# A decoder layer on one core: a written order changed in cross-attention, and 64 tokens laid out twice

## The chip, the core and the metric

The kernel runs on one core of a Trainium2 chip. A core has a matrix engine (TensorE, PE in the profile, with its weight loads shown apart as PEld), a vector engine (VectorE, DVE), a scalar engine (ScalarE, ACT), a general engine (GpSimd, POOL) and SyncE (SP), which here only issues transfers (DMAs). Each engine works through its own queue in order; semaphores make one wait for another. The metric is the device time of one execution in microseconds (us); lower is better.

## The reference

A post-norm decoder layer on 32 sequences of 64 tokens, so 2048 tokens of 512 features, all in float32:

```python
x = layernorm(x + attn(x))            # 32 heads, 8 key/value heads, head size 128
x = layernorm(x + xattn(x, ctx))      # the same head counts, keys and values from ctx
x = layernorm(x + ffn(x))             # z = x W + b, plus a clamped low-rank part

def attn(x):
    q, k, v = x @ wq.T, x @ wk.T, x @ wv.T         # rope on q and k, one angle set for all tokens
    k_full = concat([k_cache[block_idx], k[0]])    # 512 cached keys, then the 64 of sequence 0
    v_full = concat([v_cache[block_idx], v[0]])
    return softmax(q @ k_full.T / sqrt(128)) @ v_full @ wo.T

def xattn(x, ctx):                                 # per sequence, 64 queries by 64 keys
    q = x @ Wq + bq
    k, v = split(ctx @ Wkv + bkv)
    return softmax(q @ k.T / sqrt(128)) @ v @ Wo + bo
```

Two facts matter here: in self-attention every query sees the new keys and values of the first sequence alone (`k[0]`, `v[0]`), and cross-attention ends with the bias `bo`, added before the second layer norm.

## The kernel before

Tokens are worked on in four blocks of 512 (`tb` 0 to 3). The residual stream of a block lies in SBUF as `acc[tb]`, token rows by features, in four tiles of 128 rows; its transpose, features by tokens, is `xT[tb]`. Most matrix products of 512 by 512 by 512 are done in Strassen's manner (Winograd's form): seven products of quarter size instead of eight, numbered 1 to 7, each made by `Product.mul` as eight TensorE instructions of 256 columns (L318). The sums that go into them are made on POOL (`left_sums`, `right_sums`, `token_sums`, `output_sums`); the sums that come out are made on DVE as products leave PSUM, the matrix engine's output memory. Products share PSUM banks x, y and z, so that product 7, which adds to the bank of product 6, has to wait until DVE has read product 6 (L359), and product 4 waits for the read of product 7 (L363). The last reads of a query block add the bias (L339).

**Self-attention** goes through groups g = 0 to 7 of key/value heads, in each through the four blocks, in each through four heads. Its order on PE, DVE and ACT is that of the written program. For each group `new_keys` (L618 on) makes the keys and values of the first sequence. The keys take four matmuls of `wk` by `x64`, the 64 tokens of the first sequence, features by tokens (L628). The values are wanted twice, on partitions 0 to 63 and on 64 to 127 of one bank, since they are used in pairs of heads with half of the array each; so `x64` is the weights side of eight matmuls (L634), four feature chunks times two halves of the output partitions. (Each float32 matmul shows as two instructions in the trace, so 16 in a call.) `x64` is copied out of the first block's transpose once at the start, on POOL (L820). `cached_keys` (L648) and the score matmuls (L667) come behind `new_keys` on PE.

**The key/value stage** makes the keys and values of the context for all of cross-attention, in four passes `gp` over four blocks, seven products each (L426, L432; DVE reads L443). PE and DVE follow the written order; POOL, ACT and SP are placed by the scheduler. Between the products a list `fill` is worked off, one entry after each product: the statistics and scaling of the first layer norm in pass 1, and from pass 2 the turning of `acc` into `xT`, four DVE transposes a block (`turn_rows`, L149) and 16 small transfers (`move_rows`, L156). Empty entries space the blocks out.

**Cross-attention** goes through 32 units, `units[n] = (g, tb)`, eight groups by four blocks. PE, POOL and DVE follow the written order (until the last unit, from which DVE is placed by the scheduler). The loop from L1347 does in iteration n, in this order:

- the queries of unit n: products 1, 6, 5, 7, 2, 4, 3, each followed by its DVE read, with pending scalings (`scales`) let in behind the read of product 6, and the token sums for unit n + 1 on POOL (`next_tokens`, L1317 to L1322);
- what is pending from a layer norm (`scales`, then `later`, which turns a finished block), with `a_turn` putting single transposes between products;
- `attend(n - 1)`: weighted values (L1191), which need the transposed softmax weights `pTx` that eight transfers of `move(n - 1)` (L1169, on SP) bring; their eviction, half by ACT (L1210) and half by DVE (L1212); `output_sums` on POOL (L289 to L295);
- `scores(n)` (L1119), the largest score (L1128);
- in group 0 alone, the bias: four POOL adds of `bo` to `acc[tb]` (L1398), one for each tile of 128 rows;
- the output projection of unit n - 1, products 1, 5, 6, 3, 7, 2, 4 (L318, DVE reads L387 and L395), with the softmax steps of unit n between them: exponentials (L1135, L1136), denominators (L1140), weights (a reciprocal L1144 and a multiply L1145, for halves 0 and 1), then the turn of both halves (L1155) and `move(n)`;
- with the last block of a group, `load_xq(g + 1)`: loads of the next query weights and their four sums on POOL (L223 to L226).

In unit 0 there is no projection, so its softmax stands alone between its scores and unit 1's queries. In group 7 the projection of a block is its last, and `layernorm_parts` follows at once (L1223 on): `stats()` makes the statistics on DVE (L173 to L175) and the square root on ACT (L176); `scale`, left in `scales`, makes a reciprocal and a shift on DVE (L187, L189) and scales the four tiles on ACT (L191).

Of the kernel before, what the change touches and what calls it, by code (L numbers as in the profile page):

```python
# [9 lines left out]
F32 = mybir.dt.float32  # L10
I32 = mybir.dt.int32
AF = mybir.ActivationFunctionType
ALU = mybir.AluOpType
# [3 lines left out]
P = 128  # L17
# [4 lines left out]
SEQ = 64  # L22
TB = 512
NTB = NT // TB
TPB = TB // P
NC = DIM // P
# [26 lines left out]
def decoder_layer(  # L53
# [30 lines left out]
    nc = tc.nc  # L84
# [431 lines left out]
    with ExitStack() as ph:  # L516
# [97 lines left out]
            nc.vector.tensor_tensor(k4[:, :, :, 0], k4[:, :, :, 0], tmp, ALU.add)  # L614


        x64 = kc.tile([P, NC, SEQ], F32, name="x64")

        def new_keys(g):

            wk, wv = wkv_cur.pop(g)
            kTs[g] = kv.tile([P, NKEY], F32, tag="kT", name=f"kT{g}")
            new = bank([P, 1, TB], f"new{g}", "po1")[:, 0, :]
            pk, pv = new[:, :SEQ], new[:, P : 2 * P]
            for c in range(NC):
                nc.tensor.matmul(  # L628
                    pk, wk[:, c, :], x64[:, c, :], start=(c == 0), stop=(c == NC - 1),
                    skip_group_check=True,  # L630
                )
            for c in range(NC):
                for i in range(2):
                    nc.tensor.matmul(  # L634
                        pv[i * SEQ : (i + 1) * SEQ, :], x64[:, c, :], wv[:, c, :],
                        start=False, stop=(c == NC - 1), skip_group_check=True,
                    )
            nc.scalar.activation(
                kTs[g].rearrange("p (s b k) -> p s b k", s=2, k=SQ)[:, :, SHARED, :],
                pk.rearrange("p (s k) -> p s k", s=2), AF.Copy, scale=nrm2,  # L640
            )
            nc.scalar.copy(vs[g][:, NKT, :], pv)
# [174 lines left out]
        t = {i: big.tile([P, 2, HF], F32, tag=f"tx{i}", name=f"tx0_{i}") for i in range(1, 5)}  # L817
        for j in range(NKT):
            gather_keys(0, j)
        nc.gpsimd.tensor_copy(  # L820
            x64.rearrange("p c (j k) -> p c j k", j=TPB),
            xTs[0].rearrange("p c (j k) -> p c j k", j=TPB)[:, :, :, : SEQ // TPB],
        )
        nc.vector.tensor_tensor(t[1], q[0, 1], q[0, 0], sub)
        nc.vector.tensor_tensor(wq0[7], wq0[1], wq0[5], sub)
        nc.vector.tensor_tensor(wq0[5], wq0[5], wq0[4], ALU.add)
# [187 lines left out]
    with ExitStack() as ph:  # L1014
# [23 lines left out]
        with ExitStack() as st:  # L1038
            ke = st.enter_context(tc.tile_pool(name="ke", bufs=1))
            psum.append(st.enter_context(tc.tile_pool(name="kps", bufs=1, space=PSUM)))  # L1040
            st.enter_context(tc.manual_schedule(
                engines={mybir.EngineType.PE, mybir.EngineType.DVE}
            ))
            for tb in range(2, NTB):
                encT[tb] = ke.tile([P, NC, TB], F32, tag=f"encT{tb}", name=f"encT{tb}")
                load_features(encT[tb], encT_in, tb)
            kvw[1] = load_kv_left(1, "wo")
            fill = []

            pairs = [(gp, tb) for gp in range(NKV // 2) for tb in range(NTB)][1:]  # L1050
            for k, (gp, tb) in enumerate(pairs):
                if gp == 1:
                    stats, scale = layernorm_parts(tb, "a")
                    fill += [lambda: None, stats, lambda: None, scale]
                if gp == 2:
                    room = ke.tile([P, DIM // SQ, SQ, TPB], F32, tag="room", name=f"room{tb}")
                    fill += [lambda tb=tb, j=j, room=room: turn_rows(
                        acc[tb][:, j, :], room, j) for j in range(TPB)]
                    fill.append(lambda tb=tb, room=room: move_rows(room, xT[tb]))

                    fill += [lambda: None] * 7
                tiles = [ke.tile([P, 2, 2, HF], F32, tag=f"c{i}", name=f"c{gp}_{tb}_{i}", bufs=2)
                         for i in range(2)]
                pr = keys_values(gp, tb, tiles, {z: f"{z}{k % 2}" for z in "xyz"})
                for i in KV_ORDER:
                    pr.step(i)
                    pr.read()
                    if fill:
                        fill.pop(0)()
                if gp == 0 and tb < NTB - 1:  # L1070
                    encR[tb + 1] = token_sums(
                        encT[tb + 1], f"te{tb + 1}", nc.gpsimd, ke, f"te{tb + 1}_"
                    )
                store_kv(gp, tb, tiles)
                if tb == NTB - 1 and gp < 2:
                    kvw[gp + 2] = load_kv_left(gp + 2, ("wq", "wo")[gp])
                if tb == NTB - 1 and gp == 2:
                    load_xq(0)
                if gp == 3 and tb == 0:
                    right[0] = token_sums(xT[0], "txx0", nc.gpsimd)  # L1080
            load_xo(0)
            psum.pop()
# [134 lines left out]
        def project(n, *steps):  # L1217
            g, tb = units[n]
            for i in steps:
                pjs[n].step(i)  # L1220
                pjs[n].read()
            if steps[-1] == 4:
                del pjs[n]  # L1223
                if g == NKV - 1:
                    stats, scale = layernorm_parts(tb, "x", by_act=True)
                    stats()
                    scales.append(scale)
                    if tb < 2:
                        later.append(lambda: turn_block(tb))
                    else:  # L1230
                        later.append(lambda: transpose_block(tb, "x2"))
# [104 lines left out]
        def parts(n, *made):  # L1336

            for part, pr in made:
                if n < N:
                    part(n, pr)  # L1340

        def steps(n, *made):
            if n >= 0:
                project(n, *made)

        mxs, es, dens, scales = {}, {}, {}, []
        for n in range(N + 1):  # L1347
            if n == N - 1:

                units_order.close()  # L1350
                ph.enter_context(tc.manual_schedule(
                    engines={mybir.EngineType.PE, mybir.EngineType.Pool}
                ))
            if n < N:
                g, tb = units[n]
                q = queries(n)
                for i in (1, 6, 5, 7):
                    q.step(i)
                    q.read()
                    while scales and i == 6:  # L1360
                        scales.pop(0)()
                q.corner()
                q.step(2)


                behind = g > 0 and tb == 1
                if not behind:
                    next_tokens(n + 1, 0)
            while scales:
                scales.pop(0)()  # L1370
            while later:
                later.pop(0)()
            if n < N:
                a_turn()
                q.step(4)
                q.read()
                a_turn()
                q.step(3)
                q.read()
                a_turn()  # L1380


            if n > 0:
                attend(n - 1)
            if n < N:
                if n + 1 < N:
                    load_kv(n + 1)
                scores(n)
                if behind:
                    next_tokens(n + 1, 0)  # L1390
                next_tokens(n + 1, 1)
            if n == N:
                feed_forward(1)
            parts(n, (largest, 0), (largest, 1))
            if n < N and g == 0:
                for j in range(TPB):
                    a = acc[tb][:, j, :]
                    nc.gpsimd.tensor_tensor(a, a, bo, ALU.add)  # L1398
            steps(n - 1, 1, 5)
            parts(n, (exponentials, 0))  # L1400
            steps(n - 1, 6)
            parts(n, (exponentials, 1), (denominators, 0))
            a_turn()
            steps(n - 1, 3)
            parts(n, (denominators, 1))
            if n < N and tb == NTB - 1 and g + 1 < NKV:
                load_xq(g + 1)
            steps(n - 1, 7)
            parts(n, (weights, 0))
            steps(n - 1, 2)  # L1410
            parts(n, (weights, 1))
            if n > 0:
                steps(n - 1, 4)
                parts(n, (turn, 0), (turn, 1))
                if n < N:
                    move(n)
                if n < N and tb == 0:
                    if g > 0:
                        load_xo(g)
                    if g == NKV - 1:  # L1420
                        load_ffn()
            if n == 0:
                parts(n, (turn, 0), (turn, 1))
                move(n)
            if n == N - 1:
                feed_forward(0)
        scales.pop(0)()
# [51 lines left out]
```

## Time and profile before

| what | us |
|---|---|
| three runs | 3034.66, 3035.4, 3037.62 (median 3035.4) |
| the profiled execution | 3034.3 |
| its span, first to last instruction | 3032.2 |
| PE busy | 3005.9 |
| DVE busy | 2187.9 |
| POOL busy | 961.5 |
| ACT busy | 801.7 |

By time: self-attention ends near 1838, the key/value stage runs to 2023, cross-attention to about 2980, where it overlaps with the feed-forward network that ends the kernel. The granted TensorE clock is 0.999 of full speed. A line of the wait view names the engine and line that waited, what it waited for, the total, the number of times and the longest. A line of the chain view gives start, duration, engine, tile and line. A line of the timeline has start, duration, engine, line, operation, tiles and shapes, and in brackets how long the engine had idled before it and for whom. All starts are in us from the beginning of the span. Instructions of one engine overlap a little, so the distance between two starts, not the duration, tells what one costs: a quarter product of eight instructions is 1.89 from first start to last end and 1.73 from start to start.

### The profile page before, as it was taken

To read this page: it belongs to the slowest core of one execution; us is meant where nothing else is said; L and a number is where in the kernel's file an instruction comes from. 1 tells how busy PE (TensorE), PEld (TensorE's weight loads), DVE (VectorE), ACT (ScalarE), POOL (GpSimd) and SP (SyncE) were. 2 spreads that over 40 slices of the span, in tenths; PEclk is the share of its full clock that TensorE was granted. 3 is DMA by queue.
4 is the path that set the end of the run, shared out by engine and by line. 5 is a ranking of instruction groups with operands and counts; after the bars stand their busy time and mean duration, and the time that the engine had idled before them with its cause. 6 is when DMAs were issued, how large, how long until landed. Compare 5 with 4: busy or idle time off the path is not lost.

```text
span 3032.2 us, 42610 instructions
## 1 busy us (share of the span) xinstructions
PE 3005.9 (99%) x14848; PEld 2318.4 (76%) x14848; DVE 2187.9 (72%) x4045; ACT 801.7 (26%) x1916; POOL 961.5 (32%) x798
## 2 busy tenths in 40 slices
PE   8999999999999999999999999999999999999998
PEld 6777777777777777777777768988888888888875
DVE  6787777777877877877877863547666666666787
ACT  4322222222232332232232231111111111111233
POOL 5222321321321321321321223035444444444320
PEclk9999999999999999999999999999999999999999
DMA  6454444444444444444444344341121121121121
GB/s 182 129 133 126 114 111 126 114 110 126 113 111 126 112 112 125 111 113 127 109 115 116 93 132 146 129 145 54 50 67 53 52 66 51 56 63 50 55 58 42
DMA packets 216084, 304.99 MB, mean 101 GB/s; under 512 B 47424, under 2 KB 110400, under 8 KB 215872
## 3 DMA queue, kind: packets, MB, share of 16 engines
q1 hardware_dynamic: 201584, 286.91, 34.7%
q10 hardware_dynamic: 11472, 9.46, 1.0%
q0 software_dynamic: 2816, 5.90, 0.7%
q8 instruction: 120, 1.97, 0.3%
q14 instruction: 92, 0.75, 0.1%
HBM read 107.05 MB, written 20.97 MB: 42 GB/s over the span
## 4 chain that ended last, share of the span: by engine, by line
PE 96%; DVE 2%; DMA 1%; POOL 0%; ACT 0%; issue 0%; ACTq 0%; DVEq 0%; POOLq 0%
PE po L718 16%; PE s L667 16%; PE sx L1119 2%; PE pox L1191 2%; PE w_1y L318 1%; PE q_3y L318 1%; PE w_0y L318 1%; PE w_3y L318 1%; PE q_1y L318 1%; PE q_0y L318 1%; PE qx_0y L318 1%; PE wx_0y L318 1%; PE qx_3y L318 1%; PE wx_3y L318 1%; PE wx_1y L318 1%; PE q_2y L318 1%
## 5 line engine op out<-in xcount | busy, mean ns | idle before, releaser
L675 ACT ACTIVATE p<-s,nmax 128x576 f32<-128x576 f32 x512 | 379.1, 740 | 1211.3 <-DVE nmax L672 1166.6
L667 PE MATMUL s<-kT,qT 128*128 128x288 f32 x2048 | 575.3, 407 | 0.5 <-ACT p L675 0.5
L718 PE MATMUL po<-pT,v 128*128 128x512 f32 (+1 forms) x1280 | 549.1, 602 | 2.5 <-DMA wv<-in_wvT 1.4
L667 PEld LDWEIGHTS s<-kT,qT 128*128 128x128 f32 x2048 | 387.7, 190 | 101.6 <-issue 19.7
L672 DVE TENSOR_REDUCE nmax<-s 128x1 f32<-128x576 f32 x512 | 383.5, 749 | 60.6 <-PE s L667 59.6
L698 DVE STREAM_TRANSPOSE T<-p 128x576 f32<-128x576 f32 x512 | 393.9, 769 | 11.7 <-ACT p L688 7.4
L718 PEld LDWEIGHTS po<-pT,v 128*128 128x128 f32 (+1 forms) x1280 | 213.3, 189 | 202.5 <-issue 175.3
L690 DVE TENSOR_SCALAR p<-p,den 128x576 f32<-128x576 f32 x488 | 305.3, 626 | 17.1
L684 DVE RECIPROCAL den<-den 128x1 f32<-128x1 f32 x512 | 83.8, 164 | 225.7 <-ACT p L675 214.2
L289 POOL TENSOR_TENSOR so<-oT,oT 128x512 f32<-128x512 f32 x32 | 40.7, 1272 | 543.3 <-ACT oT L741 543.3
L292 POOL TENSOR_TENSOR so<-oT 128x512 f32<-128x512 f32 x32 | 40.6, 1270 | 310.3 <-PE w_1y L318 92.8
L289 POOL TENSOR_TENSOR sox<-oTx,oTx 128x512 f32<-128x512 f32 x32 | 40.5, 1266 | 296.8 <-ACT oTx L1210 210.5
L1210 ACT ACTIVATE oTx<-pox,bv 128x128 f32<-128x128 f32 x256 | 73.7, 488 | 117.2 <-PE pox L1191 117.2
L230 POOL TENSOR_TENSOR tx<-xT 128x512 f32<-128x512 f32 x31 | 40.5, 1306 | 197.5 <-PE q_3z L318 63.3
L675 ACT ACTIVATION_READ_ACCUMULATOR p<-s,nmax 128x1 f32 x512 | 98.7, 193 | 0.0
L1320 POOL TENSOR_TENSOR txx<-x1T 128x512 f32<-128x512 f32 x31 | 39.3, 1268 | 175.1 <-PE qx_3z L318 75.3
L1136 ACT ACTIVATE ex<-ex 128x512 f32<-128x512 f32 x64 | 40.3, 630 | 202.2 <-DVE ex L1135 202.2
L1212 DVE TENSOR_SCALAR oTx<-pox,bv 128x128 f32<-128x128 f32 x256 | 72.6, 421 | 8.5 <-PE pox L1191 8.5
L1119 PEld LDWEIGHTS sx<-kvx,qTx 128*64 128x64 f32 x2048 | 62.3, 138 | 10.6 <-issue 10.6
L741 ACT COPY oT<-po 128x512 f32<-128x512 f32 x128 | 68.2, 586 | 4.5 <-PE po L718 4.1
L1119 PE MATMUL sx<-kvx,qTx 128*64 128x64 f32 x2048 | 66.7, 224 | 0.0
L1191 PE MATMUL pox<-pTx,kvx 64*128 64x256 f32 x512 | 64.6, 389 | 0.3 <-DMA pTx<-Tx 0.3
(445 smaller groups left out, 5773.1 us busy)
## 6 DMA issues: line engine op xcount, KB each, us to landing
pT<-T SPq DMA_DIRECT2D x1016, 80.0 KB
pT<-T SPq DMA_DIRECT2D x1008, 64.0 KB
xT<-in_xT SPq DMA_DIRECT2D x123, 256.0 KB
kvx<-kv SPq DMA_DIRECT2D x32, 512.0 KB
pTx<-Tx SPq DMA_DIRECT2D x256, 64.0 KB
kv<-c SPq DMA_DIRECT2D x30, 512.0 KB
wo<-in_woT SPq DMA_DIRECT2D x32, 256.0 KB
xwq<-in_xwq SPq DMA_DIRECT2D x32, 256.0 KB
```

What stands on the lines that cost most here:

```text
L289: nc.gpsimd.tensor_tensor(t[1], a[1, 0], a[1, 1], ALU.add)
L318: nc.tensor.matmul(self.banks[b][:, m, :], self.left[i][:, k, m * P : (m + 1) * P], self.right[i][:, k, :], start=(first and m + k == 0), ...
L667: nc.tensor.matmul(s[:, a, :HALF], qTs[n // REP][:, units[n][2], i * P : (i + 1) * P], kTs[g][:, a * HALF : (a + 1) * HALF], start=True, s ...
L672: nc.vector.tensor_reduce(nmax, s[:, :, :HALF], AX.XY, ALU.max, negate=True)
L675: nc.scalar.activation(p.rearrange("q (a k) -> q a k", a=2), s[:, :, :HALF], AF.Exp, bias=nmax, accum_out=den,)
L684: nc.vector.reciprocal(den, den)
L690: nc.vector.tensor_scalar(p, p, den, None, ALU.mult)
L698: nc.vector.transpose(Ts[n][:, :, i, :], ps_.pop((n, i)).rearrange("q (b k) -> q b k", k=SQ))
L718: nc.tensor.matmul(pos[n].rearrange("d (a q) -> d a q", a=NQD), vs[units[n][0]][rows, v, :], pTs[n // 2][rows, :, chunk, :], skip_group_ch ...
L1119: nc.tensor.matmul(s[b * SEQ : (b + 1) * SEQ, i * REP + h, :], qTs[n][:, h, pr * HF + c0 : pr * HF + c0 + SEQ], kvs[n][:, pr, 0, c0 : c0 + ...
L1191: nc.tensor.matmul(po[pr, b][:, i, :].rearrange("d (h a j) -> d h a j", h=REP, a=2), kvs[n][r, pr, 1, i * HD : (i + 1) * HD], pTs[n][r, :, ...
L1210: nc.scalar.activation(dst, src, AF.Identity, bias=bias)
```

## The change

Four things change, none of which alters what is computed.

1. The tokens of the first sequence lie twice in `x128`, side by side, copied by two POOL copies. The new values are then four matmuls with 128 columns of weights, whose output fills all 128 partitions, instead of eight with 64.
2. The bias adds go from units 0 to 3 of cross-attention into the `fill` list of the key/value stage, one entry for a block's four adds, right behind the transfers that move the block's transpose. An empty entry makes room for it.
3. In unit 0 the second half of the weights step, both turns and `move(0)` are put into a list `due`, which is worked off in unit 1 behind the DVE read of product 6.
4. In group 7 the statistics of block 0 go into `due` too, so they run in unit 30 behind the read of product 6; the scalings of all blocks are no longer let in at that place and run behind product 2, where the loop has emptied `scales` all along.

In the changed program's built order, DVE differs at two places (units 1 and 30), ACT at one (in unit 30 the eviction L354 goes ahead of the scaling L191), POOL in the second copy and the 16 adds, and SP nowhere.

```diff
-        x64 = kc.tile([P, NC, SEQ], F32, name="x64")
+        x128 = kc.tile([P, NC, 2 * SEQ], F32, name="x128")
+        x64 = x128[:, :, :SEQ]
...
             for c in range(NC):
-                for i in range(2):
-                    nc.tensor.matmul(
-                        pv[i * SEQ : (i + 1) * SEQ, :], x64[:, c, :], wv[:, c, :],
-                        start=False, stop=(c == NC - 1), skip_group_check=True,
-                    )
+                nc.tensor.matmul(
+                    pv, x128[:, c, :], wv[:, c, :],
+                    start=False, stop=(c == NC - 1), skip_group_check=True,
+                )
...
-        nc.gpsimd.tensor_copy(
-            x64.rearrange("p c (j k) -> p c j k", j=TPB),
-            xTs[0].rearrange("p c (j k) -> p c j k", j=TPB)[:, :, :, : SEQ // TPB],
-        )
+        for i in range(2):
+            nc.gpsimd.tensor_copy(
+                x128[:, :, i * SEQ : (i + 1) * SEQ].rearrange("p c (j k) -> p c j k", j=TPB),
+                xTs[0].rearrange("p c (j k) -> p c j k", j=TPB)[:, :, :, : SEQ // TPB],
+            )
...
+            def add_bias(tb):
+                for j in range(TPB):
+                    a = acc[tb][:, j, :]
+                    nc.gpsimd.tensor_tensor(a, a, bo, ALU.add)
...
                     fill.append(lambda tb=tb, room=room: move_rows(room, xT[tb]))
+                    fill.append(lambda tb=tb: add_bias(tb))
-                    fill += [lambda: None] * 7
+                    fill += [lambda: None] * 6
...
                     stats, scale = layernorm_parts(tb, "x", by_act=True)
-                    stats()
+                    if tb == 0:
+                        due.append(stats)
+                    else:
+                        stats()
                     scales.append(scale)
...
+        due = []
         mxs, es, dens, scales = {}, {}, {}, []
...
                 for i in (1, 6, 5, 7):
                     q.step(i)
                     q.read()
-                    while scales and i == 6:
-                        scales.pop(0)()
+                    while due and i == 6:
+                        due.pop(0)()
...
             parts(n, (largest, 0), (largest, 1))
-            if n < N and g == 0:
-                for j in range(TPB):
-                    a = acc[tb][:, j, :]
-                    nc.gpsimd.tensor_tensor(a, a, bo, ALU.add)
             steps(n - 1, 1, 5)
...
             steps(n - 1, 2)
-            parts(n, (weights, 1))
             if n > 0:
+                parts(n, (weights, 1))
                 steps(n - 1, 4)
...
             if n == 0:
-                parts(n, (turn, 0), (turn, 1))
-                move(n)
+                due += [lambda: parts(0, (weights, 1), (turn, 0), (turn, 1)), lambda: move(0)]
```

## The prediction

> **What bounds the kernel now.** I read the busy times first, then the chain of work that ended last, then PE's waits from the start of cross-attention on.
>
> ```profile
> PE 3005.9 (99%) x14848; PEld 2318.4 (76%) x14848; DVE 2187.9 (72%) x4045; ACT 801.7 (26%) x1916; POOL 961.5 (32%) x798
> PE 96%; DVE 2%; DMA 1%; POOL 0%; ACT 0%; issue 0%; ACTq 0%; DVEq 0%; POOLq 0%
> PE qx_0y L318 <- POOL xwq L225: 1.8, 1, 1.8
> PE qx_1y L318 <- DVE qTx L359: 1.5, 1, 1.5
> PE qx_2y L318 <- DVE rstd_x L187: 1.2, 1, 1.2
> ```
>
> TensorE is the bound nearly everywhere: other engines matter only where PE stands still. In 1000 us of cross-attention and feed-forward it stands still three times for more than a microsecond, and the change has one edit for each. The fourth edit shortens PE's own work, in self-attention. So the sum has four terms, each a place on PE's line.
>
> **Term A, new values with full width (new_keys).** Eight calls, seven in steady state. In the chain, one of them reads (start, duration, what):
>
> ```profile
> 1243.89 0.97 PE s L667 x4
> 1246.59 0.84 PE new L628 x8
> 1247.42 1.02 PE new L634 x16
> 1248.45 1.17 PE s L667 x4
> 1997.09 0.89 PE kv_1z L432 x8
> ```
>
> The sixteen half-wide instructions of L634 (64 columns of weights) take 1.02 us. The score matmuls right behind them take 1.17, where the same four take 0.97 elsewhere: leaving the half-wide form costs 0.20. After the change there are eight instructions of 128x128 weights by 128 columns; the row of exactly that shape is the last one, 0.89 for eight, with no change of form on either side. Gain per call 1.02 - 0.89 + 1.17 - 0.97 = 0.33 us. In the first call the instructions behind are four transposes, 0.59 there against 4 x 0.11 = 0.44 in later groups, so 0.28. Sum 7 x 0.33 + 0.28 = 2.6 us. PE has no wait at these places, so all of it counts; bounds 0 (the form makes no difference; a loss is excluded by the 0.89 row, which no half-wide row undercuts) and 8 x 0.33 = 2.7. The second POOL copy costs another 0.79 (L820's duration) between 9.9 and 13.0 us, where POOL idles 3.08 us for gathered keys; PE first reads the copy at 15.1. Without that idle it would delay the key rotation by 0.79 at most.
>
> The Trainium skill, "TensorEngine Tiling (Array Packing)", section Theoretical Speedup, speaks against this edit: a side of at most 64 lets two tiles work at once, up to 2x. By that the halves already filled the array and A would be the 0.20 behind them alone, some 1.5 us in all; the rows give sixteen halves 1.02 against 0.89 and so bear it out for most of the time, not all.
>
> **Term B, the bias adds leave POOL's queue.** Sixteen adds of 1.27 us (L1398), four in each of units 0 to 3. In unit 3 they stand ahead of the four sums for the next query weights:
>
> ```profile
> 2118.43 4.95 POOL L1398 TENSOR_TENSOR acc<-acc,bo 128x512 f32<-128x512 f32 x4
> 2126.83 1.26 POOL L225 TENSOR_TENSOR xwq<-xwq,xwq 128x512 f32<-128x512 f32 x1
> 2128.14 1.99 PE L318 MATMUL qx_0y<-txx,xwq 128*128 128x256 f32 x8 [1.75 <-POOL xwq L225]
> ```
>
> PE's products follow each other every 1.73 us; the one before started at 2124.50 and the one after at 2129.98, so the stop cost 5.48 - 2 x 1.727 = 2.03 us. Without the adds L225 ends near 2122, 4 us ahead of need; the weights' transfers were issued at 2105 to 2107 and the transfer engines are quiet by 2110. Next in line is unit 4's weighted-value product, whose transposed weights land near 2134.5 against a need at 2136.7: covered. B = 2.0 (bounds 1.9 to 2.1). In their new place, the key/value stage, the adds take 16 x 1.27 = 20.3 us of a POOL that idles there in three stretches of about 40 us. Behind them in POOL's new order stand weight sums and the first token sums; the latter ended at 1985.3 and are read at 2025. Each add waits for the DVE transposes of its block, all done by 1996.2; DVE touches acc again at 2057.8. Cost 0; were POOL not idle, 20 us less that slack of 40.
>
> **Term C, unit 0's second half of the softmax behind the first read of unit 1.** Today:
>
> ```profile
> 2042.65 1.30 DVE L1155 STREAM_TRANSPOSE Tx<-ex 128x512 f32<-128x512 f32 x2
> 2043.87 0.65 DVE L359 TENSOR_TENSOR qTx<-qx_1y,qTx 128x512 f32<-128x512 f32 x1
> 2043.97 5.21 SPq L1169 DMA_DIRECT2D pTx<-Tx  x8
> 2044.67 1.97 PE L318 MATMUL qx_1y<-txx,xwq 128*128 128x256 f32 x8 [1.55 <-DVE qTx L359]
> 2051.74 2.00 PE L1191 MATMUL pox<-pTx,kvx 64*128 64x256 f32 x16
> ```
>
> The stop costs (by starts, 2041.23 to 2046.47) 5.24 - 3.45 = 1.79. With L359 moved ahead of reciprocal, multiply and two transposes, product 7 follows at once, and PE reaches the weighted values (L1191) at 2049.95. But the transposes now end 0.61 us later (one L359), and with them all eight transfers of move(0) start 0.61 later. How long they take shows in unit 31, where PE caught up with them: issue from 2899.08, the first two matmuls at 2904.58, the rest held until 2905.60.
>
> ```profile
> 2905.60 1.96 PE L1191 MATMUL pox<-pTx,kvx 64*128 64x256 f32 x14 [0.32 <-DMA pTx<-Tx]
> ```
>
> That is 2.1 us after the eighth transfer's issue (2903.5). In unit 0 the eighth goes out at 2048.6, so the data are there at 2050.7, and after the change at 2051.3. PE stops again, and the scores start 1.89 after that (2905.60 to 2907.49), at 2053.2 where they started at 2053.67. C = 0.5 net; bounds 0.1 (landing 0.4 later) and 1.79 (no stop). SP's order is unchanged, and nothing else is queued there between 2044 and 2053.
>
> **Term D, unit 30's statistics behind the transposes and the first read.** The stop is worth 1.42 (starts 2866.12 to 2870.99, less 3.45). In the new DVE order the two transposes run first, L359 at 2866.4, then the 3.5 us of statistics, then L363 at 2870.5, ending near 2871.2, just when PE wants its bank (2871.3). Two reads of 0.44, reciprocal and shift follow; ACT scales the first tile from 2872.6 to 2873.35. From there DVE alternates three turns of 1.05 and two reads of 0.8: 2873.45 + 4.75 = 2878.2, and only then can it evict the weighted values (L1212). Today:
>
> ```profile
> 2878.12 2.16 DVE L1212 TENSOR_SCALAR oTx<-pox,bv 128x128 f32<-128x128 f32 x8
> 2880.43 1.26 POOL L289 TENSOR_TENSOR sox<-oTx,oTx 128x512 f32<-128x512 f32 x1 [7.91 <-DVE oTx L1212]
> 2882.04 1.89 PE L318 MATMUL wx_1z<-xwo,sox 128*128 128x256 f32 x8
> ```
>
> L289's sum ended at 2881.69 and PE's weight load for wx_1z began at 2881.83: under 0.1 us of slack. DVE comes to L1212 no earlier than before, so PE gains 1.4 and hands it back at wx_1z. D = 0 (bounds -0.5, if L363 makes PE stop as well, and 1.42).
>
> **Sum.** 2.6 + 2.0 + 0.5 + 0 = 5.1 us. The profiled execution took 3034.3 (span 3032.2), so 3029.2; the median of the runs lies 1.1 above it, so 3030.3.
>
> **Rivals.** (1) The new stops don't come: C and D in full, 2.6 + 2.0 + 1.8 + 1.4 = 7.8, time 3027.6. For it: both of my stops rest on margins of about a microsecond put together from many rows. Against: unit 31 shows the landing directly.
> (2) The doubled tokens don't do what they say: 128-column weights cost 0.19 a load against 0.137 (L628 and L634), and if loads set the pace A is 0: 5.1 - 2.6 = 2.5, time 3032.9. Against: the L432 row, the same shape, back to back.
> (3) Slower: POOL and DVE stand in each other's way in the key/value stage. For it: beside the adds, a DVE multiply with both operands in SBUF took 1.85 us where 0.69 is its median.
>
> ```profile
> 2119.59 0.68 DVE L387 TENSOR_TENSOR acc<-wx_2z,acc 128x512 f32<-128x512 f32 x1
> 2122.08 1.85 DVE L1145 TENSOR_TENSOR ex<-ex,denx 128x512 f32<-128x512 f32 x1
> ```
>
> If a run of four adds (5.1 us) held up the bank reads (L443), PE would have 0.8 us of cover (read ends 2002.28, next product on the bank at 2003.09) and lose 4.3 four times, 17.1: 3035.4 - 5.1 + 17.1 = 3047.4. It decides from 1.3 us a run. Against: L443 adds a bank to an SBUF tile, and L387, of the same form, took 0.68 with adds beside it. [...]
>
> **Chances and range.** Forecast 0.60, own range 3028.4 to 3032.2 (the terms' bounds, and a median of runs that spread over 3 us); rival 1 0.28, between its 3027.6 and the forecast if one of the stops shrinks; rival 2 0.08; rival 3 0.04. The range 3026.9 to 3032.9 leaves out rival 3, half of rival 2 and rival 1's tail. Two thousandths, 6.1 us, are about what a measurement of this kernel can tell from no change; the line is at 3029.3, 1.0 below the forecast. Faster: rival 1 and a third of the forecast, 0.48; within: the rest and rival 2, 0.48; slower: 0.04.
>
> **What would show it.** A: eight instructions in 0.89 and score matmuls of 0.97 behind them. B: no PE wait on L225, and an early POOL. C: PE's wait moves from L359 to L1191 on pTx, about 1 us. D: the wait on L187 is gone, one of 1.0 to 1.4 stands at wx_1z on POOL's sum. Wrong would be: no such new waits (rival 1), 1.0 us still at the new values (rival 2), or PE waits in the key/value stage (rival 3).

## The result, and the profile after

The median went from 3035.5 us (22 runs) to 3032.06 (22 runs), a ratio of 0.9985 with a 95% interval of 0.9979 to 0.9990: 3.4 us by the medians. The forecast was 3030.3. The kernel's times now lie in two groups, eleven of them between 3028.1 and 3031.2 and eleven between 3032.9 and 3036.1, so the median is the middle of a gap in which no run lies; the profiled execution (3033.54, span 3031.7) is one of the second group, and the same kernel profiled again in the first experiment (3030.37, span 3028.5) is one of the first. Both are needed to see what happened, so here is the time between marks on PE's line, in us (sx n is the first score matmul of unit n in cross-attention):

| from, to | before | after | after, again |
|---|---|---|---|
| first query product to first new values | 10.34 | 12.23 | 11.50 |
| to the key/value stage | 1822.54 | 1819.92 | 1820.44 |
| key/value stage | 185.54 | 185.55 | 185.54 |
| to sx 0 | 12.25 | 12.25 | 12.26 |
| sx 0 to sx 1 (term C) | 18.01 | 20.23 | 17.58 |
| sx 1 to sx 3 | 56.62 | 56.68 | 56.62 |
| sx 3 to sx 4 (term B) | 30.33 | 28.31 | 28.31 |
| sx 4 to sx 29 | 707.83 | 707.83 | 707.83 |
| sx 29 to sx 30 (term D) | 29.73 | 28.57 | 28.57 |
| sx 30 to sx 31 | 29.29 | 30.86 | 30.50 |
| sx 31 to the end | 124.68 | 124.22 | 124.22 |

The first line lies between 10.34 and 12.23 in all fourteen profiles taken. In five of them, both of the table's after columns included, the kernel's second product took 3.78 us, in the other nine 1.99; the line is 11.50 to 12.23 in those five and 10.34 to 11.42 in the nine. There is only one profile of the kernel before, the shortest of all, so whether the second POOL copy adds to this line is not shown. The busy times and PE's waits from cross-attention on are now:

```profile
PE 3007.7 (99%) x14784; PEld 2321.4 (77%) x14784; DVE 2184.7 (72%) x4045; ACT 801.9 (26%) x1916; POOL 961.5 (32%) x799
PE pox L1199 <- DMA pTx<-Tx: 3.1, 2, 1.8
PE wx_1x L318 <- DVE oTx L1220: 0.4, 1, 0.4
```

All three waits that the prediction started from (on L225, L359 and L187) are gone. In their place PE waits twice at the weighted values (L1191 before, now L1199) for the transposed weights, and once for an eviction (L1212, now L1220). And PE is busy 1.8 us longer than before although it has 64 instructions fewer: something made instructions longer. Part of it is the start: the second and third products took 3.78 and 2.45 us here, 1.99 each before. The rest is found under term C. Term by term:

**A.** The chain of waits at the same new values that the prediction showed (start, duration, what):

```profile
1246.94 0.84 PE new L630 x8
1247.78 0.95 PE new L635 x8
1248.72 0.97 PE s L668 x4
```

The score matmuls are at 0.97, as forecast; the eight full-width instructions take 0.95, not 0.89. So 1.02 + 1.17 - 0.95 - 0.97 = 0.27 a call, and the distance from one call to the next fell by the same 0.27 (226.26 to 225.99). In the first call the transposes behind fell from 0.59 to 0.44, so 0.22 there. A = 7 x 0.27 + 0.22 = 2.1. By starts on PE's timeline the 0.27 is shared otherwise: keys, values and scores took 0.93, 1.03 and 1.07 before and take 0.83, 0.95 and 0.97 now, so about 0.1 lies at each change of form, ahead of the values as well as behind them.

**B.** The timeline of POOL and PE around unit 4's first products:

```profile
2120.03 1.27 POOL L223 TENSOR_TENSOR xwq<-xwq,xwq 128x512 f32<-128x512 f32 x1
2122.74 1.27 POOL L225 TENSOR_TENSOR xwq<-xwq,xwq 128x512 f32<-128x512 f32 x1
2127.83 1.89 PE L318 MATMUL qx_0y<-txx,xwq 128*128 128x256 f32 x8
```

The sums follow each other on POOL without the adds, L225 ends at 2124.0 and the product that reads it starts at 2127.83 with no wait in brackets: 3.8 us of cover. B = 30.33 - 28.31 = 2.02.

**C.** The timeline of unit 1 on DVE, SP and PE:

```profile
2041.13 0.68 DVE L359 TENSOR_TENSOR qTx<-qx_1y,qTx 128x512 f32<-128x512 f32 x1
2042.57 1.30 DVE L1163 STREAM_TRANSPOSE Tx<-ex 128x512 f32<-128x512 f32 x2
2043.89 6.29 SPq L1177 DMA_DIRECT2D pTx<-Tx  x8
2049.28 0.70 PE L1199 MATMUL pox<-pTx,kvx 64*128 64x256 f32 x2
2051.74 3.54 PE L1199 MATMUL pox<-pTx,kvx 64*128 64x256 f32 x14 [1.77 <-DMA pTx<-Tx]
```

L359 is early and the query products run on, as planned. But the eight transfers took SP 6.29 us to issue (5.21 before: one of them took 1.67 where the median is 0.59), so PE stood still for 1.77 us. And then the fourteen weighted-value instructions took 3.54 us where unit 31's took 1.96. The table by windows of the same place says why (window, its length, then busy time and number of instructions of PE, weight loads, DVE, ACT and POOL, then the granted TensorE clock, the DMA share and GB/s):

```profile
2049.00:2052.00 3.00, 1.23 (x6) 0.58 (x6) 0.87 (x2) 0.00 (x0) 0.00 (x0) 0.99 0.29 70
2052.00:2055.00 3.00, 3.00 (x14) 2.37 (x12) 1.21 (x4) 1.72 (x6) 0.00 (x0) 0.50 0.00 0
2055.00:2058.00 3.00, 3.00 (x68) 2.67 (x68) 2.43 (x6) 0.80 (x4) 1.27 (x1) 0.94 0.55 167
```

From 2051.97 to 2055.38 TensorE was granted half its clock. That is the other part of the lengthening of PE's busy time, and together with the late transfer it turned a gain of 0.43 (the other execution) into a loss of 2.2.

**D.** Around unit 30, the timeline of PE, DVE and SP:

```profile
2871.06 1.97 PE L318 MATMUL qx_2y<-txx,xwq 128*128 128x256 f32 x8
2877.28 2.20 DVE L1220 TENSOR_SCALAR oTx<-pox,bv 128x128 f32<-128x128 f32 x8
2879.11 1.97 PE L318 MATMUL wx_1x<-xwo,oTx 128*128 128x256 f32 x8 [0.41 <-DVE oTx L1220]
2887.67 11.27 SPq L156 DMA_DIRECT2D x1T<-room  x16
2899.04 5.01 SPq L1177 DMA_DIRECT2D pTx<-Tx  x8
2905.58 1.96 PE L1199 MATMUL pox<-pTx,kvx 64*128 64x256 f32 x14 [1.29 <-DMA pTx<-Tx]
```

Unit 30's scores come 1.16 sooner (28.57 against 29.73). Some 0.6 is handed back at once, since DVE is late with the eviction: wx_1x starts 2.50 behind the scores instead of 2.02, and wx_1z takes 0.1 longer. The rest goes in unit 31. There the eight transfers of `move(30)` stand in SP's queue behind the sixteen that carry block 0's transpose. SP went through these in 11.27 us (10.31 before), reached `move(30)` at 2899.04, where it had done so at 2899.08, and PE waited 1.29 for the data instead of 0.32.

### The profile page after: what moved, and what is told of

Its sections match the earlier page's. It is cut to its first block, busy times and chain, and to the rows that moved or that the text cites. A ratio compares the mean times of both kernels' runs of the same rounds, so it can differ in the third digit from the quotient of the medians.

```text
span 3031.7 us, 42481 instructions
## 1 busy us (share of the span) xinstructions
PE 3007.7 (99%) x14784; PEld 2321.4 (77%) x14784; DVE 2184.7 (72%) x4045; ACT 801.9 (26%) x1916; POOL 961.5 (32%) x799
## 4 chain that ended last, share of the span: by engine, by line
PE 96%; DVE 2%; SPq 1%; DMA 1%; ACT 0%; issue 0%; ACTq 0%; DVEq 0%
PE po L719 16%; PE s L668 16%; PE sx L1127 2%; PE pox L1199 2%; PE w_0y L318 1%; PE q_2y L318 1%; PE q_3y L318 1%; PE w_3y L318 1%; PE q_1y L318 1%; PE q_0y L318 1%; PE wx_3y L318 1%; PE wx_2y L318 1%; PE wx_0y L318 1%; PE qx_0y L318 1%; PE wx_1y L318 1%; PE w_2y L318 1%
## 5 line engine op out<-in xcount | busy, mean ns | idle before, releaser
L289 POOL TENSOR_TENSOR so<-oT,oT 128x512 f32<-128x512 f32 x32 | 40.7, 1272 | 545.4 <-ACT oT L742 545.4
L289 POOL TENSOR_TENSOR sox<-oTx,oTx 128x512 f32<-128x512 f32 x32 | 40.5, 1266 | 300.7 <-ACT oTx L1218 209.5
L1220 DVE TENSOR_SCALAR oTx<-pox,bv 128x128 f32<-128x128 f32 x256 | 72.8, 422 | 12.8 <-PE pox L1199 12.8
L1127 PEld LDWEIGHTS sx<-kvx,qTx 128*64 128x64 f32 x2048 | 62.4, 138 | 10.9 <-issue 10.3
L1199 PE MATMUL pox<-pTx,kvx 64*128 64x256 f32 x512 | 66.8, 396 | 3.1 <-DMA pTx<-Tx 3.1
```

Source lines behind the costliest of these rows:

```text
L289: nc.gpsimd.tensor_tensor(t[1], a[1, 0], a[1, 1], ALU.add)
L1127: nc.tensor.matmul(s[b * SEQ : (b + 1) * SEQ, i * REP + h, :], qTs[n][:, h, pr * HF + c0 : pr * HF + c0 + SEQ], kvs[n][:, pr, 0, c0 : c0 + ...
L1199: nc.tensor.matmul(po[pr, b][:, i, :].rearrange("d (h a j) -> d h a j", h=REP, a=2), kvs[n][r, pr, 1, i * HD : (i + 1) * HD], pTs[n][r, :, ...
```

## The experiments

All of them change the changed kernel, unless another base is named. The first four ran on one chip beside 32 runs of the kernel before (median 3036.23).

**The same kernel again.** No edit.

> The changed kernel again. Its 22 times lay in two groups, about 29.7 and 33.3 past 3000, those of the kernel before in one. Theory: the upper group are executions in which the eight transfers of unit 0's move come late and PE stops in unit 1 for about 3 us; the profile then shows that stop (3.1 us in two pieces) if its time is near 3033, and one of at most 1.2 us if it is near 3030. Rival: the groups come from the first 20 us (landing of the first loads); then the stop in unit 1 is the same in both and the new values' first matmul starts 2 us later in the upper one.

Median 3030.2 (11 runs), ratio 0.998 [0.9971, 0.9989]. Nine of the eleven times lie between 3029.3 and 3031.4, two at 3032.7 and 3033.1; the profiled one, 3030.37, is of the nine. In this profiled execution the transfers of unit 0 were issued in the usual time, and PE's next instructions show what the mechanism of term C costs when nothing else happens (timeline of SP and PE):

```profile
2043.79 5.21 SPq L1177 DMA_DIRECT2D pTx<-Tx  x8
2050.56 1.96 PE L1199 MATMUL pox<-pTx,kvx 64*128 64x256 f32 x14 [0.69 <-DMA pTx<-Tx]
```

The eighth transfer goes out near 2048.4 and PE goes on 2.1 us later; that is the time to the landing, when the data are in place, which the prediction took from unit 31. PE waits 0.69, keeps its clock (1.96 for the fourteen), and C is 18.01 - 17.58 = 0.43.

**The change without C.** Unit 0's softmax, turn and transfers are back in unit 0:

```diff
+            parts(n, (weights, 1))
             if n > 0:
-                parts(n, (weights, 1))
...
-                due += [lambda: parts(0, (weights, 1), (turn, 0), (turn, 1)), lambda: move(0)]
+                parts(n, (turn, 0), (turn, 1))
+                move(n)
```

> Only unit 0's softmax goes back to its old place, so the move starts 0.6 us earlier against the products and PE has its old 1.6 us stop at the read of product 6. Theory: one group of times, about 2.1 (new values, 0.27 x 7 + 0.22 as the changed trace has it) + 2.0 (bias) + 0.6 (unit 30) = 4.7 under the kernel before, near 3030.8, and never 3033 because of unit 1. Rival: two groups as before, 3.6 us apart.

Median 3029.95 (11 runs), ratio 0.9978 [0.9969, 0.9987], against 0.998 [0.9971, 0.9989] with C. PE waits 1.55 on L359 again and sx 0 to sx 1 takes 18.01. One transfer of unit 0 was issued late here too (eight in 6.19 us), yet PE did not wait for it: late issues come without C as well, and what C took away is the time that covered them. So C as it was written has no measurable worth: what it gains when all goes well it loses when a transfer is late.

**C with its transfers on two queues.** The eight transfers of `move(0)` go out alternately from SP's and ACT's queues:

```diff
-        def move(n):
+        def move(n, queues=(nc.sync,)):
...
-                        nc.sync.dma_start(
+                        queues[a % len(queues)].dma_start(
...
-                ... lambda: move(0)]
+                ... lambda: move(0, (nc.sync, nc.scalar))]
```

> The change with unit 0's eight transfers issued in turn from two queues (SyncE and ScalarE), four each, so that issue takes half as long and the last one leaves about 2.3 us earlier. Theory: PE's stop at the weighted values of unit 1 is gone, all 1.8 us of term C are kept, one group of times near 3035.5 - 2.1 - 2.0 - 1.8 - 0.6 = 3029.0. Rival: still two groups.

The timeline of SP, ACT's queue and PE in unit 1:

```profile
2045.29 2.48 SPq L1177 DMA_DIRECT2D pTx<-Tx  x4
2045.30 2.77 ACTq L1177 DMA_DIRECT2D pTx<-Tx  x4
2050.68 2.00 PE L1199 MATMUL pox<-pTx,kvx 64*128 64x256 f32 x16
```

Four transfers a queue are issued in 2.5 to 2.8 us instead of eight in 5.2, the data are there when PE comes, all sixteen instructions run in one piece, and sx 0 to sx 1 takes 16.23: C is 1.78, the whole of the stop that was removed. Median 3027.81 (10 runs), ratio 0.9971 [0.9962, 0.9981]. What cost C its gain is thus the issuing of eight transfers one after another, not the moved DVE work as such. The profile shows this; the time alone does not, since its interval overlaps with that of the changed kernel.

**A alone**, on the kernel before: only the doubled tokens and the full-width matmuls.

> Only the doubled tokens. Each of eight calls: values 0.95 where sixteen halves took 1.02, and 0.97 where 1.17 followed: 2.1 us in all, so about 3033.4, one group. Rival (the prediction's sum): 2.6.

Median 3033.5 (11 runs), ratio 0.9992 [0.9983, 1.0001], 2.7 us under the kernel before by the medians, but the interval reaches no change. The profile decides: the same 0.95 and 0.97 at each call, all three later waits as before (1.8, 1.6, 1.2), the same 185.55 in the key/value stage.

The next four ran together on one chip beside 26 runs of the kernel before (median 3036.22); their base is the two-queue kernel.

**Block 0's sixteen transfers on two queues as well.**

```diff
-    def move_rows(room, dst):
+    def move_rows(room, dst, queues=(nc.sync,)):
...
-                nc.sync.dma_start(
+                queues[r % len(queues)].dma_start(
...
-            turns.append(lambda: move_rows(room, xT[tb]))
+            queues = (nc.sync, nc.scalar) if tb == 0 else (nc.sync,)
+            turns.append(lambda: move_rows(room, xT[tb], queues))
```

> The kernel of the two-queue run, and besides the 16 transfers x1T<-room of the first token block go alternately out on SP's and ACT's queues. Theory (the rest of term D's gain was handed back behind these 16 transfers on SP, 10.9 us of issuing that ends 0.1 us before move(30) can start): move(30) starts to issue when the transposes end, near 2895.0, the wait at the weighted values of unit 31 shrinks from 0.9 us to 0.3 or less, and from unit 30's scores to unit 31's it takes 29.6 to 30.0 us where it took 30.5; time 0.5 to 0.9 us under the two-queue kernel, about 3027.0. Rival (the transposes, late behind the statistics of the second block, set the landing, not the queue): the wait stays at 0.8 to 0.9 us, the time is that of the two-queue kernel.

Timeline of SP, ACT's queue and PE:

```profile
2885.02 6.59 SPq L156 DMA_DIRECT2D x1T<-room  x8
2884.98 6.89 ACTq L156 DMA_DIRECT2D x1T<-room  x8
2895.05 5.00 SPq L1177 DMA_DIRECT2D pTx<-Tx  x8
2900.94 2.60 PE L1199 MATMUL pox<-pTx,kvx 64*128 64x256 f32 x16
```

SP is free at 2891.6, `move(30)` starts the moment the transposes end (2895.0), and the sixteen instructions run without a wait in brackets, in 2.60 instead of 2.00. sx 30 to sx 31 takes 29.55, where the two-queue kernel took 30.47 and 30.84 in its two profiles. So the rest of D was indeed handed back behind those sixteen transfers. The time, 3029.51 (10 runs), ratio 0.9977 [0.9967, 0.9986], is not the 3027.0 that was expected, and can't be told from that of the two-queue kernel beside it (3029.79); a gain of 1.0 us is under the scatter.

**The two-queue kernel without D.** Block 0's statistics at once, as before:

```diff
-                    if tb == 0:
-                        due.append(stats)
-                    else:
-                        stats()
+                    stats()
```

> The kernel of the two-queue run with the statistics of the first token block back where they were before the change, ahead of the transposes and of the first read. Theory (term D is worth nothing on balance): PE waits 1.2 us on L187 again in unit 30 and takes 29.7 us from unit 29's scores to unit 30's instead of 28.6; but the two waits of 0.1 to 0.4 at wx_1x and wx_1z go, and from unit 29's scores to unit 31's it is 59.0 to 59.6 us either way; time within 0.5 us of the two-queue kernel. Rival (D gains what its first half shows): 1.2 us slower than the two-queue kernel.

PE waits 1.18 again, and sx 29 to sx 30 is back at 29.74. Over both units, sx 29 to sx 31, this execution took 60.11; the kernels without D took 59.02, 59.57 and 60.11 (mean 59.57), the ten profiles with D and block 0's transfers on SP alone 59.03 to 59.64 (mean 59.40). So D is worth 0.2 with a scatter of 0.5. The median was 3030.85 (11 runs), ratio 0.9983 [0.9974, 0.9992], 1.1 over the two-queue kernel: more than the theory's 0.5 allowed, but the intervals overlap, and the time alone doesn't tell zero from the rival's 1.2. The profiles speak for zero.

**Stops of many lengths.** To see from what length a stop of PE costs clock, idle multiplications on DVE hold up the read on which product 7 waits, in twelve units:

```diff
                     q.step(i)
+                    if i == 6:
+                        for _ in range(STOPS.get(n, 0)):
+                            nc.vector.tensor_tensor(idle, idle, idle, ALU.mult)
                     q.read()
```

> The kernel of the two-queue run with idle work added on DVE: multiplications of a 128x512 tile of zeros by itself, 5 to 12 of them ahead of the second read of the queries in twelve units of cross-attention (units 6, 7, 10, 11, 14, 15, 18, 19, 22, 23, 26, 27 with 5, 6, 7, 8, 9, 10, 6, 7, 8, 9, 10, 12), so that PE stands still at L318 for about 0.7 us with 5 and 0.6 us more for each further one. Theory (a stop of TensorE of somewhat over 2 us halves the granted clock for the next 3 us or so): after the stops up to about 1.8 us the products behind follow at 1.73 us each, after those from about 2.4 us on one or two of them take 3.4 us, 1.5 to 1.7 us lost a stop; time of the whole 3027.8 plus the stops' 25 to 35 us plus 8 to 14 us. Rival (the half clock in unit 1 of the changed kernel came from something else, such as the short weighted-value products or the transfers): the products behind follow at 1.73 after stops of every length.

Timeline lines of PE at three of the stops:

```profile
2190.03 1.97 PE L318 MATMUL qx_2y<-txx,xwq 128*128 128x256 f32 x8 [0.98 <-DVE qTx L359]
...
2221.15 2.52 PE L318 MATMUL qx_3y<-txx,xwq 128*128 128x256 f32 x8 [2.56 <-DVE qTx L359]
2223.45 3.10 PE L318 MATMUL qx_3x<-x1T,xwq 128*128 128x256 f32 x8
...
2348.69 3.68 PE L318 MATMUL qx_3y<-txx,xwq 128*128 128x256 f32 x8 [4.96 <-DVE qTx L359]
2352.20 1.89 PE L318 MATMUL qx_3x<-x1T,xwq 128*128 128x256 f32 x8
```

and the windows behind the last of them (columns as above):

```profile
2344.00:2348.60 4.60, 0.00 (x0) 0.00 (x0) 4.53 (x4) 0.00 (x0) 2.68 (x2) 1.00 0.48 128
2348.60:2351.60 3.00, 2.91 (x7) 2.38 (x8) 0.03 (x1) 0.00 (x0) 0.00 (x0) 0.53 0.00 0
2351.60:2354.60 3.00, 3.00 (x14) 2.54 (x14) 1.57 (x3) 0.47 (x2) 1.27 (x1) 0.90 0.00 0
```

The stop of 0.98 left the clock alone. Each of the eleven stops from 2.56 to 7.86 us was followed by half clock, which covered 2.9 to 6.1 us of the work behind it and cost half of that, 1.4 to 3.0 us, on top of the stop. The cost does not grow steadily with the length (2.56 cost 1.7, 6.51 cost 1.5, 7.86 cost 3.0). The rival falls: half clock comes without short weighted-value products beside the stop. Transfers ran during the stop shown (a DMA share of 0.48), so their part is not tested by itself. The time, 3115.49, lies far above what was expected, since the stops came to 57 us instead of 25 to 35: the idle multiplications, one SBUF tile by itself, took 0.69 in the median but up to 1.64. The stops jumped from 0.98 to 2.56, so this run says nothing about the lengths between.

**The two-queue kernel again**, in the same batch.

> The kernel of the two-queue run once more, beside the others on the same chip: 3027.8 +- 0.8 us if its earlier median holds, in a ratio of 0.996 to 0.998 to the kernel before. From unit 0's scores to unit 1's 16.2 us again, the whole of term C; with the changed kernel's own 17.6 to 20.2 us instead, that gain was chance.

Median 3029.79 (11 runs), 1.2 above the range that was expected; ratio 0.9977 [0.9968, 0.9986]. sx 0 to sx 1 took 16.49, and 16.96 and 16.63 in the two kernels built on it. So C gains 1.0 to 1.8 with two queues in these four profiles; the issues took 2.5 and 2.8 us in all four, and what varies is the landing, which stretches the sixteen weighted-value instructions from 2.00 to 2.3 to 2.7. Only the kernel with the stops is an exception: there a table load of 1.28 us on ACT came ahead of unit 0's exponentials, both queues needed 3.9 us, and sx 0 to sx 1 took 18.55. And the medians of one and the same kernel moved by 2 us from batch to batch.

**Four more profiles of the changed kernel**, one execution each, to see whether its two groups of times come from unit 1.

> The changed kernel as it is, one profiled execution of four. Theory (its times lie in two groups about 3.6 us apart because the new stop at the weighted values of unit 1 sometimes passes the length from which TensorE's clock halves): where unit 1 takes 17.5 to 18.3 us from unit 0's scores to its own, the clock stays at 1.0 behind the stop and the execution takes 3028 to 3031.5 us; where it takes 19.5 or more, a window of 3 us behind the stop shows about 0.5 and the execution takes 3032.5 to 3036. Rival (the groups come from the start of the kernel or from elsewhere): unit 1's length and the time do not go together.

Times 3035.11, 3030.44, 3030.2 and 3030.05; sx 0 to sx 1 took 19.95, 17.59, 18.26 and 17.58. With the two profiles above (3033.54 with 20.23, 3030.37 with 17.58) all six fall as the theory has it; behind the stop of the long one the two windows of 3 us were granted 0.80 and 0.63. PE's timeline in unit 1 of the long one and of the 18.26:

```profile
2053.15 3.12 PE L1199 MATMUL pox<-pTx,kvx 64*128 64x256 f32 x14 [1.47 <-DMA pTx<-Tx]
```

```profile
2049.95 1.96 PE L1199 MATMUL pox<-pTx,kvx 64*128 64x256 f32 x14 [1.38 <-DMA pTx<-Tx]
```

In both, a transfer was issued late (eight in 6.43 and in 5.88 us). The stop of 1.38 cost itself alone; that of 1.47, with 0.40 of standing still just ahead of the first two instructions, cost half clock too. Unit 1 is not the whole of it: the long one also stood still for 2.55 us near 66 us, in self-attention, where PE waits for transposed weights in every kernel, and lost another 1.7 of clock there. Nor are times in groups peculiar to this kernel: those of A alone, whose unit 1 is that of the kernel before, lie in two (seven from 3031.8 to 3033.7, four from 3035.5 to 3037.2), and six of the two-queue kernel's first ten lie from 3026.8 to 3027.8, the other four from 3030.1 to 3033.7.

## Why the prediction was right or wrong

**Term A, the mechanism right, the size 2.1 instead of 2.6.** The term that was mis-sized is the 0.89 for eight full-width instructions. That row (L432) stands behind products of 256 columns. Behind the four key matmuls of L630, of 64 columns, the same shape took 0.95; the 0.06 a call is 0.5 in eight. The 0.20 behind the values went, as forecast, although by starts half of it lies ahead of them. Rival 2 falls at every call. Of the 0.27 a call, 0.07 is at the values themselves and 0.20 behind them, as the chain view counts. The Trainium skill's rule ("TensorEngine Tiling (Array Packing)", Theoretical Speedup), that two halves already share the array, was as near as the row: by the rule A was 1.5, by the row 2.6, and the runs, at 2.1, lie midway.

**Term B, right**: 2.02 against 2.0, with no cost in the new place. The adds ran in the key/value stage, PE had no wait there but the 0.8 at its start that it had before, the stage took 185.55 against 185.54, and the bank reads beside the adds (L443) stayed at 0.69. That is also the end of rival 3.

**Term C, right in its mechanism, wrong in its range.** The stop on L359 went, a new one on `pTx` came, 2.1 us after the eighth issue as worked out, and where the issues took their usual 5.2 us C was 0.43 against 0.5. The step that failed is the lower bound: 0.1, "landing 0.4 later", as the worst. It took the 5.21 of one profile for the time of eight issues. In six profiles of the changed kernel the eight took from 5.2 to 6.4 us, and since the step had put PE right at the landing, each late issue counts; behind a long enough stop comes half clock, for which the sum had no term. The profile before gave no row for its price: its stops of 1.2 to 1.8 us kept their clock, and half clock stands there only from 3025.49 on, where PE has ended. C was 0.4 in three of six profiles, -0.25 in one, -1.9 and -2.2 in two: on average -0.5, not 0.5.

**Term D, right in its sum, half wrong in its way.** It is nothing on balance, as forecast. But the prediction let the whole of it come back at wx_1z, on POOL's sum (L289). Only about 0.6 did, most of it one step sooner, at wx_1x on DVE's eviction (L1220 started 29.24 us behind unit 29's scores, at 2877.28; the 2878.2 worked out was 29.74 behind them). The rest came back a unit later, on SP. The step that failed was to follow DVE and POOL only: the transposes that D moves feed sixteen transfers, and these stand ahead of `move(30)`.

**The sum.** Where no transfer is late 2.1 + 2.0 + 0.4 + 0 = 4.5; with half clock in unit 1, 2.1 + 2.0 - 2.1 + 0 = 2.0. With the mean C of the six profiles it is 2.1 + 2.0 - 0.5 + 0 = 3.6. The forecast's 5.1 is above all three, and the median of the 22 runs, with half of them in the later group, was 3.4 below the kernel before. That it lies inside the range of 3026.9 to 3032.9 is partly luck: the range has nothing in it for half clock, and one more run in the later group would have made the median 3032.93, just past its end. Rival 1, that the new stops don't come, is out for the kernel as it is, and is what the two-queue kernels made true for C. What stays open: the medians of the repeated runs (3030.2 for the changed kernel, 6.0 below the kernel beside it) differ by more than the pieces give, and by up to 2 us between batches for one and the same kernel. Where unit 1 is not the cause, the start of the kernel has a part in it (the stop near 66 us was 1.4 to 2.9 us long over all profiles). The key/value stage began at 1835.8 to 1838.5 us in the six profiles of the changed kernel and at 1837.9 in the one before, so the scatter up to there is larger than term A; what makes it was not tested.

**The best version run** is the two-queue kernel, 3027.81 and 3029.79 in its two batches (ratios 0.9971 and 0.9977), with or without the split of block 0's transfers. It is the best by its medians; its intervals overlap with that of the change without C.

## What to carry to other kernels

When a stop is removed by moving work that feeds small transfers, follow it to the last transfer and its landing, and ask how far the issues of that queue vary, not only how long they took once: an engine put right at a landing pays for every late issue. Splitting a run of such transfers over two queues took all or most of the landing off the path in four profiles of five. And price a stop of the matrix engine with what follows it: by starts, one of 1.18 us cost 1.4 and one of 2.56 cost 4.5.

## What the runs showed of the hardware

**The clock behind a stop.** All fourteen stops of 2.55 us or more behind the start of the kernel were followed by half clock and lost 1.4 to 3.0 us to it, median 1.7. Stops of 1.18 to 1.76 as a single piece were not. Between, it goes both ways: one of 2.34 kept its clock, as the timeline line of PE near 66 us in the second of the four further profiles shows, while unit 1's 1.77 right behind a short run of two instructions lost it.

```profile
66.29 1.96 PE L719 MATMUL po<-pT,v 128*128 128x512 f32 x4 [2.34 <-DMA pT<-T]
```

In the two-queue kernel's profile the same place, after a stop of 2.73, reads:

```profile
66.57 3.61 PE L719 MATMUL po<-pT,v 128*128 128x512 f32 x4 [2.73 <-DMA pT<-T]
```

The length of the stop is not all that counts. In every one of these traces the granted clock changes at moments that lie whole multiples of 3.41 us apart, and half clock lasts one such window or several: in the run with stops 3.41 us six times, 6.83 four times and 10.24 once, part of it inside the stop. If the traces are cut at these moments, all 28 windows at full clock in which PE was busy for 1.34 us or less were followed by half clock, none with 1.67 or more was, and between 1.47 and 1.66 both occur. So it matters how a stop falls into the windows. That of 1.77 lay whole in one, with 1.64 us of work in it (columns as above):

```profile
2048.56:2051.97 3.41, 1.64 (x8) 0.91 (x8) 0.87 (x2) 0.00 (x0) 0.00 (x0) 1.00 0.33 79
2051.97:2055.38 3.41, 3.41 (x17) 2.57 (x17) 1.27 (x5) 2.10 (x8) 0.00 (x0) 0.50 0.00 0
2055.38:2058.79 3.41, 3.41 (x71) 3.19 (x72) 2.47 (x6) 0.42 (x2) 2.03 (x2) 1.00 0.50 154
```

The Trainium skill, "TensorE: Matmul & The Clock Gate", Part 1, has the array's clock fall to half after at least one idle window of about 3.4 us, in windows that run freely whatever the kernel does. Half clock and windows that run freely agree with these traces; that a window has to be idle does not, since windows with up to 1.34 us of work sufficed every time. An estimate by that page: one window of 3.41 us at half speed loses 1.7 us and two lose 3.4; measured were 1.4 to 3.0, with part of the half clock inside the stops.

**Issuing small transfers.** Eight of 64 KB took one queue 4.9 to 6.4 us; four on each of two queues took 2.5 to 2.8, and once 3.9. Sixteen of block 0's took one queue 10.3 to 11.5 us and two queues 6.9: the gain is less than twofold there. Why a single issue now and then takes 1.3 to 2.1 us, where the median is 0.59, is not shown.
